# Three stacked attention passes over a graph: the copies of turned rows move from VectorE to ScalarE and wait longer, and a row sum is added up by accumulating transfers

## The chip, the cores and the metric

The kernel runs on one core of one Trainium2 chip, in fp32. The metric is the device time of one execution in microseconds (us); the number given for a kernel is the median of several runs. A profile is one execution taken by the hardware profiler; its span is the time from the first to the last instruction, and its own time is a little longer. The engines are called PE (TensorE), ACT (ScalarE), DVE (VectorE), POOL (GpSimd) and SP (SyncE, which here issues nearly all transfers).

## The reference, cut to what matters

Four residual layers over N = 3327 nodes with 256 features; `adj` is a dense 0/1 matrix. The first three are a cosine attention, a GAT and a query-key attention. The fourth, which the change concerns, is three GAT passes one after the other:

```python
def _gat_layer(h, adj, W, a):
    Wh = h @ W
    f1 = Wh @ a[:F_out]
    f2 = Wh @ a[F_out:]
    e = leaky_relu(f1 + f2.T, ALPHA)
    att = softmax(where(adj > 0, e, NEG_INF), axis=1)
    return elu(att @ Wh)

h = input @ W0
h = _gat_layer(h, adj, W1, a1)      # pass "3a"
h = _gat_layer(h, adj, W2, a2)      # pass "3b"
h = _gat_layer(h, adj, W3, a3)      # pass "3c"
x = layernorm(x + h)
```

## The kernel before, in words

**Tiling.** The nodes are padded to 3328 and cut into 26 tiles of 128 (NT). The rows of the result are cut into 7 blocks (NB): six of 512 (four tiles) and a last one of 256 (two tiles). For a block b and a tile j of source nodes, the attention weights are a 128 x 512 tile. A layer goes over its blocks; in each block over the 26 tiles, in steps j = 0 to 25; PE adds the product of the weights and the tile's values (with a column of ones for the softmax's denominator) into PSUM.

**The weights** of one tile: ACT computes a Relu (L787, `re`), and DVE adds and multiplies by the mask (L800, `ft`). In the deep passes (3a, 3b, 3c; `deep(L)`) four tiles lie in a quad, of which there are three. The weights are made some steps ahead of the products.

**The products** follow Strassen's scheme (`products`, L935) in all blocks of a deep pass but the last: a pair of tiles takes 14 matmuls of 128 x 128, which show as 28 records, instead of 16. For this DVE makes sums of the weights (`quad_sums`, L871 to L874, `qsum`; `sums`, L885, `ssum`), and sums of the values (`combine`, L843 to L853) are stored to memory once per pair of tiles, when the values are made in the pass before; SP fetches them again for each block (`fetch_tsum`, L857, three buffers). The column of ones in such a sum is set by a POOL memset (L843).

**The end of a block** is a generator, `finish`. It runs beside the next block's products, one `yield` per step j (and is run to its end at j = 22). Its parts in a deep pass are: DVE and ACT put the Strassen parts together (`joined`, L961 to L979); ACT divides by the denominators (L1175, L1177); `turn` transposes the block's rows: two ACT copies split the fp32 words into two planes of 16 bits (L990), SP issues a DMA transpose (L993), some yields go by, and two DVE copies put the words together again (L1000, `pT`). PE then projects each of the four tiles by the weights of the pass (L1230, `pproj`, two matmuls a tile); ACT makes the exponential and the Relu of elu (L1239, L1242); and DVE adds them (`activated`, L1254). In the hidden passes (3a and 3b) `follow` then adds the tile to a running sum (`Sum.add`, L1084, one DVE add of 128 x 256), and takes the scores f1 and f2 of the next pass (L719); after each two tiles `combine` makes the next pass's sums. Of block NB-2 the running sum's adds are put off (`L.late`) to after the last block. `Sum.close` (L1088 to L1091) takes the sum across partitions on PE and stores the mean row in the padding row of the values; the values of the whole pass must be there for that.

**How many steps the turned rows wait** is `turn_steps`: 4 in deep passes, at block NB-2 it is 7 (9 in 3c).

**Buffers.** The planes, `pT4` and the tile sums of `combine` share a tag of two buffers ("x4k"). The turned rows lie in one of four "stage" buffers, the elu's exponential in one of two.

**What sets the order.** The code is written as one stream: the step loop calls weights, products and one `advance` of the finishes. A scheduler at build time orders the instructions of each engine's queue from it and places the waits. On the chip each engine works through its queue in order, so an instruction that waits holds up all behind it on that engine.

Of the kernel before, what the change touches and what calls it, by code (L numbers as in the profile page):

```python
# [14 lines left out]
ALU = mybir.AluOpType  # L15
# [18 lines left out]
def gnn_stack(ctx: ExitStack, tc: tile.TileContext, a: dict, N: int, out: bass.AP):  # L34
# [8 lines left out]
    nc = tc.nc  # L43
    NT = (N + P - 1) // P
    NP = NT * P
    NB = (NP + CH - 1) // CH
# [36 lines left out]
    n = 8  # L83
# [549 lines left out]
    def pair_weights(b, p):  # L633
# [16 lines left out]
        def add_two(out, x, ps):  # L650

            nc.vector.tensor_tensor(
                out.rearrange("p (i q) -> p i q", i=2),
                x.unsqueeze(1).to_broadcast([P, 2, D]),
                ps.rearrange("p (i q) -> p i q", i=2),
                add,
            )
# [46 lines left out]
    class Gat:  # L704
        def __init__(self, key):
            self.last = key == "3c"
            self.quads = ("3a", "3b", "3c").index(key) + 1 if key != "1" else 0
            self.k = w.get("k_" + key)
            self.row = w["row_" + key]
            self.sd = cols.tile([P, 2, NT], F32, tag="sd", name="sd")  # L710
            self.th = cols.tile([P, NT], F32, tag="th", name="th")
            self.rh = cols.tile([P, NT], F32, tag="rh", name="rh")
            self.nrh = cols.tile([P, NT], F32, tag="nrh", name="nrh")
            self.u = {}
# [107 lines left out]
    def deep(L):  # L822
        return L.i > 2
# [6 lines left out]
    def combine(key, p, v, e=None):  # L830


        b1, b2 = v[2 * p], v[2 * p + 1]
        b11, b12, b21, b22 = b1[:, H:D], b1[:, :H], b2[:, H:D], b2[:, :H]
        if (key, p) in kept or key == "0":
            t = work.tile([P, 4 * H + 1], F32, tag="tsum", name="tsums", bufs=3)
        else:
            t = work.tile([P, 4 * H + 1], F32, tag="x4k", name="tsum", bufs=2)
        if (key, p) in kept:
            tsums[kept[key, p], p] = t  # L840
        t1, t2, t3, t4 = (t[:, c : c + H] for c in (0, H + 1, 2 * H + 1, 3 * H + 1))
        if e is None:
            nc.gpsimd.memset(t[:, H : H + 1], 1.0)  # L843
            nc.vector.tensor_tensor(t1, b12, b11, ALU.subtract)
            nc.vector.tensor_tensor(t3, b22, b12, ALU.subtract)
        else:
            one = t[:, H : H + 1]
            nc.vector.tensor_scalar(one, e[:, :1], 0.0, None, ALU.is_ge)
            nc.vector.scalar_tensor_tensor(t1, b12, one, b11, ALU.mult, ALU.subtract)
            nc.vector.scalar_tensor_tensor(t3, b22, one, b12, ALU.mult, ALU.subtract)  # L850
        nc.vector.tensor_tensor(t2, b22, t1, ALU.subtract)
        nc.vector.tensor_tensor(t4, t2, b21, ALU.subtract)
        nc.sync.dma_start(t_d[key][p], t)  # L853
# [126 lines left out]
        return z[:, : 2 * q]  # L980


    def turn(x4, n, out, steps=3):

        half = "p k (n t) -> p t k n"
        pl = work.tile([P, 4, 2, D], U16, tag="x4k", name="planes", bufs=2)
        for t in range(2):
            nc.scalar.copy(pl[:, :n, t, :], x4[:, :n, :].bitcast(U16).rearrange(half, t=2)[:, t])  # L990
        yield
        tr = work.tile([P, 16, P], U16, tag="stage", name="turned", bufs=4)
        nc.sync.dma_start_transpose(  # L993
            out=tr[:, : 4 * n, :], in_=pl[:, :n].rearrange("p k t n -> p (k t n)")
        )
        for _ in range(steps):
            yield
        trv = tr[:, : 4 * n, :].rearrange("p (k t h) i -> p t k h i", t=2, h=2)
        for t in range(2):
            nc.vector.tensor_copy(out(t), trv[:, t])  # L1000
        yield

    def turn_steps(L, b):

        if L.key == "1":
            return 5 if b == NB - 2 else 3
        return (9 if L.key == "3c" else 7) if b == NB - 2 else 4

# [64 lines left out]
    class Sum:  # L1075


        def __init__(self):
            self.acc = cols.tile([P, D], F32, tag="xsum", name="xsum")
            nc.gpsimd.memset(self.acc, 0.0)  # L1080

        def add(self, t, x):
            r = LASTP if t == NT - 1 else P
            nc.vector.tensor_tensor(self.acc[:r], self.acc[:r], x[:r], ALU.add)  # L1084

        def close(self, v):
# [6 lines left out]
    def finish(L, b, pos):  # L1093
# [4 lines left out]
        n = len(ts_)  # L1098
# [71 lines left out]
        else:  # L1170
# [23 lines left out]
            if L.key in x_d:  # L1194
                x4 = work.tile([P, 4, D], F32, tag="stage", name="x4", bufs=4)
# [8 lines left out]
            if L.key != "2":  # L1204
                pT4 = work.tile([P, 4, 2, P], F32, tag="x4k", name="pT4", bufs=2)
                yield from turn(
                    p4,
                    n,
                    lambda t: pT4[:, :n].bitcast(U16).rearrange(
                        "p k h (i t) -> p t k h i", t=2  # L1210
                    )[:, t],
                    turn_steps(L, b),
                )
                pTs = {k: pT4[:, k] for k in range(n)}
                if L.key == "1" and b < NB - 2:
                    c4 = work.tile([P, 4, D], F32, tag="x4k", name="c4", bufs=2)
                    yield from projected4(pT4, w[L.w], c4)

            def projected(k):


                if L.key == "2":
                    src = p4[:, k, :]
                elif L.key == "1" and b < NB - 2:
                    src = c4[:, k, :]
                else:
                    pm = bank("pproj")
                    pT = pTs.pop(k)
                    for h in range(2):
                        nc.tensor.matmul(  # L1230
                            pm[:, :D],
                            pT[:, h, :],
                            w[L.w][:, h, :],
                            start=(h == 0),
                            stop=(h == 1),
                        )
                    src = pm[:, :D]
                e = work.tile([P, D], F32, tag="elu_e", name="elu_e", bufs=2)
                nc.scalar.activation(e, src, AF.Exp)  # L1239
                if L.hidden:  # L1240
                    y = work.tile([P, D], F32, tag="y", name="z", bufs=6)
                    nc.scalar.activation(y, src, AF.Relu)  # L1242
                else:
                    y = work.tile([P, D], F32, tag="y", name="y", bufs=6)
                    nc.vector.scalar_tensor_tensor(
                        y, src, 0.0, xr[k], ALU.max, ALU.add
                    )
                es[k] = e
                ys.append(y)

            def activated(k):
                e, y = es.pop(k), ys[k]
                x = nxt[ts_[k]][:, :D] if L.hidden else y
                nc.vector.scalar_tensor_tensor(x, e, 1.0, y, ALU.min, ALU.add)  # L1254
                if L.hidden:
                    follow([k], {k: x})
                else:
                    stats(k)

            for p in range(n + 2):  # L1260
                if p >= 2:
                    activated(p - 2)
                    if b == NB - 2:
                        yield
                    if L.hidden and p % 2 and b < NB - 1:
                        combine(layers[L.i + 1].key, (ts_[0] + p - 3) // 2, nxt)
                if 1 <= p <= n:
                    projected(p - 1)
                if p > 0:
                    yield  # L1270
# [186 lines left out]
    def advance():  # L1457
        while pending:
            try:
                next(pending[0])  # L1460
                return
            except StopIteration:
                pending.popleft()
# [8 lines left out]
    steps = [(L, b, j) for L in layers for b in range(NB) for j in range(NT)]  # L1472
# [79 lines left out]
    for s, (L, b, j) in enumerate(steps):  # L1552
# [146 lines left out]
        if j == NT - 1:  # L1699
            if b == 0 and not last:  # L1700
                nl = layers[L.i + 1]
                L.sum = Sum()
                if nl.is_gat:
                    if nl.key == "1":
                        while "row_1" not in w:
                            next(setup)
                    nl.gat = Gat(nl.key)
                    L.gat_next = nl.gat
            if end:
                pending.append(finish_last(pos[1:], xm, 1))  # L1710
            else:
                pending.append(finish(L, b, pos))
            advance()
# [65 lines left out]
```

## Time and profile before

| | us |
|---|---|
| median of 3 runs | 2300.66 (2299.2 to 2301.87) |
| the profiled execution, its own time | 2297.41 |
| its span | 2295.6 |
| PE busy | 2257.2 (98%) |
| PE weight loads busy | 2004.7 (87%) |
| DVE busy | 1998.3 (87%) |
| ACT busy | 1210.3 (53%) |
| POOL busy | 49.4 (2%) |

Busy times are of one profiled execution. A matmul's end is modelled in the profile and neighbouring matmuls overlap, so the busy time of PE runs ahead of what it could do at its densest pace; starts of records tell more. A group's line names engine, operation, output<-inputs and shape. "[2.23 <-DVE pT L1000]" behind a line of the timeline says that the engine sat idle for 2.23 us, until the named instruction released it. In a table of waits the three numbers are us in total, times, and the longest.

On this time scale the three deep passes lie from about 1380 us to the end: 3a to about 1690, 3b to about 2000, then 3c.

### The profile page before, as it was taken

What the parts mean: (1) busy time and instruction counts of PE and PEld (TensorE: products, weight loads), DVE (VectorE), ACT (ScalarE), POOL (GpSimd) and SP (SyncE); (2) the same over time, 40 slices, a digit from 0 to 9 for tenths busy, and PEclk for the clock granted to TensorE, in tenths of its full rate; (3) what the DMA queues carried; (4) which work ended last, traced back from release to release, by engine and by line L of the source; (5) the groups of instructions that cost most, each with busy time, mean ns of one, the idle gap of its engine ahead of it and who ended that gap; (6) DMA issues with size and microseconds to landing.
All of it is one profiled execution on the core that took longest, in us unless ns stands there. A gap on an engine that the chain in (4) does not pass through costs nothing. (4 is left out here: it accounts for less than half of the span.)

```text
span 2295.6 us, 41529 instructions
## 1 busy us (share of the span) xinstructions
PE 2257.2 (98%) x15183; PEld 2004.7 (87%) x15183; DVE 1998.3 (87%) x5437; ACT 1210.3 (53%) x1982; POOL 49.4 (2%) x196
## 2 busy tenths in 40 slices
PE   9999999999999999999999999999999999999997
PEld 7788888888888877888888899999999999999997
DVE  7789999866777777898898889999899999899996
ACT  4667777764555423223223246555666555655653
POOL 0000001000000000000000000000000000000000
PEclk9999999999999999999999999999999999999999
DMA  8655565523222322132132254444444445355542
GB/s 281 192 178 179 186 195 187 161 84 89 78 72 55 105 61 81 56 100 81 56 99 71 74 171 130 133 136 143 124 129 137 131 134 148 98 152 169 149 122 58
DMA packets 186207, 286.13 MB, mean 125 GB/s; under 512 B 80413, under 2 KB 105492, under 8 KB 181396
## 3 DMA queue, kind: packets, MB, share of 16 engines
q1 hardware_dynamic: 185732, 283.22, 41.2%
q8 instruction: 120, 1.97, 0.4%
q14 instruction: 83, 0.68, 0.1%
q10 hardware_dynamic: 272, 0.26, 0.0%
HBM read 228.21 MB, written 38.44 MB: 116 GB/s over the span
## 5 line engine op out<-in xcount | busy, mean ns | idle before, releaser
L787 ACT ACTIVATE re<-u,nrh,th 128x512 f32<-128x512 f32 (+1 forms) x728 | 539.8, 778 | 343.0 <-DVE ft L800 179.7
L1644 PE MATMUL po<-v,e 128*128 128x257 f32 x1872 | 422.3, 381 | 0.9 <-ACT p L1177 0.8
L1644 PEld LDWEIGHTS po<-v,e 128*128 128x128 f32 x1872 | 352.6, 190 | 60.9 <-issue 9.8
L935 PE MATMUL po<-tsums,qsum 128*128 128x128 f32 (+1 forms) x2520 | 352.8, 275 | 1.4 <-DMA tsums<-t3b_d 0.7
L800 DVE SCALAR_TENSOR_TENSOR ft<-re,rh,mask 128x512 f32<-128x512 f32 x468 | 341.1, 747 | 2.6 <-ACT re L787 2.6
L935 PEld LDWEIGHTS po<-tsums,qsum 128*128 128x128 f32 x2520 | 316.2, 192 | 3.5 <-DVE qsum L873 1.6
L935 PE MATMUL po<-tsums,ssum 128*128 128x128 f32 (+1 forms) x2082 | 293.2, 276 | 4.0 <-DMA tsums<-t3a_d 1.7
L935 PE MATMUL po<-v,ft 128*128 128x129 f32 x1872 | 286.1, 276 | 1.3 <-DVE p L975 0.6
L935 PEld LDWEIGHTS po<-tsums,ssum 128*128 128x128 f32 x2082 | 262.6, 192 | 7.0 <-DVE ssum L885 2.0
L935 PEld LDWEIGHTS po<-v,ft 128*128 128x128 f32 x1872 | 248.2, 192 | 4.0 <-issue 1.8
L935 PEld LDWEIGHTS po<-v,e 128*128 128x128 f32 x1196 | 172.3, 191 | 37.6 <-issue 24.9
L935 PE MATMUL po<-v,e 128*128 128x129 f32 x1196 | 185.1, 275 | 0.0
L800 DVE SCALAR_TENSOR_TENSOR e<-re,rh,mask 128x512 f32<-128x512 f32 (+1 forms) x234 | 149.1, 657 | 38.4 <-PE po L1644 28.4
L524 ACT ACTIVATE ex<-ps,rq 128x512 f32<-128x512 f32 (+1 forms) x183 | 118.9, 652 | 114.7 <-PE ps L511 109.9
L511 PE MATMUL ps<-ft 128*128 128x512 f32 (+1 forms) x364 | 166.9, 564 | 0.0
L496 DVE SCALAR_TENSOR_TENSOR e<-ex,mask 128x512 f32<-128x512 f32 (+1 forms) x182 | 115.8, 650 | 49.0 <-ACT ex L694 27.1
L935 PE MATMUL po<-tsums,ft 128*128 128x128 f32 x936 | 144.2, 275 | 0.0
L525 DVE SCALAR_TENSOR_TENSOR e<-ex,mask 128x512 f32<-128x512 f32 (+1 forms) x183 | 116.8, 644 | 31.1 <-ACT ex L524 30.5
L686 PE MATMUL ps<-gT,ft 128*128 128x512 f32 (+1 forms) x336 | 129.8, 527 | 0.0
L935 PE MATMUL po<-v,qsum 128*128 128x128 f32 x840 | 128.8, 275 | 0.0
L935 PEld LDWEIGHTS po<-tsums,ft 128*128 128x128 f32 x936 | 124.9, 193 | 0.3
L660 ACT ACTIVATE ex<-ex,off 128x512 f32<-128x512 f32 x98 | 67.0, 716 | 101.7 <-DVE ex L676 69.1
(346 smaller groups left out, 3572.8 us busy)
## 6 DMA issues: line engine op xcount, KB each, us to landing
mask<-mask_d SPq DMA_DIRECT2D x30, 1664.0 KB
stage<-in_adj_a SPq DMA_DIRECT2D x78, 512.0 KB
tsums<-t_d SPq DMA_DIRECT2D x152, 256.5 KB
tsums<-t3a_d SPq DMA_DIRECT2D x77, 256.5 KB
tsums<-t3b_d SPq DMA_DIRECT2D x77, 256.5 KB
tsums<-t3c_d SPq DMA_DIRECT2D x77, 256.5 KB
mask_d<-mask SPq DMA_DIRECT2D x6, 1664.0 KB
u<-s_d SPq DMA_DIRECT2D x24, 256.0 KB
```

Source lines behind the costliest of these rows:

```text
L496: nc.vector.scalar_tensor_tensor(e[:, :wd], t_[:, :wd], 0.0, mask(b, j), ALU.add, ALU.mult)
L511: nc.tensor.matmul(ps[:, :wd], FT[j // 4][:, 0, (j % 4) * P : (j % 4 + 1) * P], FT[b][:, 1, :wd], start=True, stop=True,)
L524: nc.scalar.activation(t_[:, c], ps[:, c], AF.Exp, scale=rq[:, j : j + 1])
L525: nc.vector.scalar_tensor_tensor(e[:, c], t_[:, c], 0.0, mask(b, j)[:, c], ALU.add, ALU.mult)
L660: nc.scalar.activation(x[k], x[k], AF.Exp, bias=off, scale=1.0 / D**0.5)
L686: nc.tensor.matmul(ps[:, :wd], FT[j // 4][:, h, (j % 4) * P : (j % 4 + 1) * P], g[:, h, :wd], start=(h == 0), stop=(h == 1),)
L787: nc.scalar.activation(t_[:, :wd], self.u[b][:, :wd], AF.Relu, bias=self.nrh[:, j : j + 1], scale=self.th[:, j : j + 1],)
L800: nc.vector.scalar_tensor_tensor(e[:, :wd], t_[:, :wd], self.rh[:, j : j + 1], mask(b, j), ALU.add, ALU.mult,)
L935: nc.tensor.matmul(o, x, y, start=(p == 0 and g not in banks[:i]), stop=(p == NT // 2 - 1 and g not in banks[i + 1 :]),)
L1644: nc.tensor.matmul(pos[k], e[:, k * P : (k + 1) * P], V[L.i % 2][i], start=(i == 0), stop=(i == NT - 1),)
```

## The change

Four edits, all concerning the deep passes:

- `turn` takes the copying function as an argument; in deep passes the two copies of turned rows (L1000) are made by ACT (`nc.scalar.copy`) instead of DVE.
- `turn_steps` is 7 for all blocks of deep passes (before: 4, and 7 at block NB-2); at block NB-2 of 3c it stays 9.
- In deep passes `finish` yields once more after each `activated`, for all blocks but the last (before: only at block NB-2).
- The running sum made in 3a and 3b is added up by transfers: for the tiles of blocks 0 to NB-3 (20 tiles a pass, 40 in all) POOL issues a transfer that adds the tile into the sum in memory on the chip (`accum_op=add`, 128 KB each). The tiles of the last two blocks are still added by DVE.

```diff
-    def turn(x4, n, out, steps=3):
+    def turn(x4, n, out, steps=3, copy=nc.vector.tensor_copy):
...
         for t in range(2):
-            nc.vector.tensor_copy(out(t), trv[:, t])
+            copy(out(t), trv[:, t])
         yield
 
     def turn_steps(L, b):
 
         if L.key == "1":
             return 5 if b == NB - 2 else 3
-        return (9 if L.key == "3c" else 7) if b == NB - 2 else 4
+        return 9 if L.key == "3c" and b == NB - 2 else 7
...
     class Sum:
-        def __init__(self):
+        def __init__(self, queued):
+            self.queued = queued
             self.acc = cols.tile([P, D], F32, tag="xsum", name="xsum")
             nc.gpsimd.memset(self.acc, 0.0)
 
         def add(self, t, x):
             r = LASTP if t == NT - 1 else P
+            if self.queued and t < 4 * (NB - 2):
+                nc.gpsimd.dma_start(out=self.acc, in_=x, accum_op=ALU.add)
+                return
             nc.vector.tensor_tensor(self.acc[:r], self.acc[:r], x[:r], ALU.add)
...
                     turn_steps(L, b),
+                    nc.scalar.copy if deep(L) else nc.vector.tensor_copy,
                 )
...
                 if p >= 2:
                     activated(p - 2)
-                    if b == NB - 2:
+                    if b == NB - 2 or deep(L) and b < NB - 1:
                         yield
...
-                L.sum = Sum()
+                L.sum = Sum(deep(L))
```

## The prediction

> **What bounds the kernel now.** I read the page's first part, then busy time by stage (windows), the tensor engine's waits, the timeline round the longest of them, and the tiles the change touches.
>
> ```profile
> PE 2257.2 (98%) x15183; PEld 2004.7 (87%) x15183; DVE 1998.3 (87%) x5437; ACT 1210.3 (53%) x1982; POOL 49.4 (2%) x196
> ```
>
> TensorE (PE) is busy for 98% of the span; VectorE (DVE) is next, ScalarE (ACT) has room. By stage (columns: window, its length, then each engine's busy time; four blocks each of layer 2, 3a, 3b and 3c, from join to join):
>
> ```profile
> core 0: us, PE busy (x) PEld busy (x) DVE busy (x) ACT busy (x) POOL busy (x), PEclk, DMA share, GB/s
> 1075.90:1247.80 171.90, 171.76 (x1069) 145.29 (x1068) 152.22 (x467) 50.58 (x94) 0.40 (x4) 1.00 0.24 76
> 1419.80:1604.50 184.70, 178.87 (x1516) 174.93 (x1515) 177.90 (x412) 108.90 (x176) 3.67 (x8) 1.00 0.46 136
> 1722.60:1909.10 186.50, 180.51 (x1511) 176.25 (x1510) 179.44 (x412) 109.74 (x175) 1.37 (x8) 0.98 0.48 135
> 2027.70:2206.30 178.60, 176.65 (x1508) 173.78 (x1507) 176.99 (x406) 106.52 (x156) 0.00 (x0) 1.00 0.52 152
> ```
>
> In 3a to 3c DVE is at 96 to 99%, beside PE at 97 to 99%: two engines at once. What PE could give: one pair of tiles starts every 3.13 us in the undisturbed stretch of 3c (2102.52, 2105.65, 2108.78), so a block of 13 pairs takes 40.7 us, and its 8 projection matmuls (16 records 0.215 us apart) 3.4: 44.1 us. Four are 176.4. The three deep windows exceed that by 8.3, 10.1 and 2.2 us. That is the prize, with the boundaries between the layers: added up over all 18 deep blocks and boundaries from the starts of PE's records, some 34 us. About 10 us more, at the entry to 3a, is not touched. The waits that make it (us in all, times, longest):
>
> ```profile
> PE pproj L1230 <- DVE pT L1000: 12.7, 13, 2.3
> PE po L935 <- DVE ssum L885: 1.4, 2, 0.7
> PE po L935 <- DMA tsums<-t3b_d: 0.9, 2, 0.7
> PE po L935 <- DVE p L975: 0.6, 2, 0.3
> ```
>
> So PE waits in 13 of the 19 finishes for the turned rows. Is DVE late with the copy, or its input? DVE's own waits, then PE and DVE at the longest case (3b, block 3):
>
> ```profile
> DVE pT L1000 <- DMA turned<-planes: 9.7, 9, 2.6
> DVE pT L1000 <- issue: 6.2, 4, 2.4
> ```
>
> ```profile
> 1828.65 0.39 PE L935 MATMUL po<-tsums,ft 128*128 128x128 f32 x2
> 1831.27 4.54 PE L1230 MATMUL pproj<-w_l_w,pT 128*128 128x256 f32 x12 [2.23 <-DVE pT L1000]
> 1835.65 0.38 PE L935 MATMUL po<-tsums,ft 128*128 128x128 f32 x2
> ```
>
> ```profile
> 1829.84 1.37 DVE L1000 COPY pT<-turned 128x1024 uint16<-128x1024 uint16 x2 [2.38 <-issue]
> ```
>
> DVE itself stood still for 2.38 us ahead of the copy: it waited for the transpose, issued at 1823.45, and the copy and PE followed. The wait is mainly the landing, not DVE's load. And three of the four projections stand together here: the 12 merged records last 4.54 us where 12 times 0.215 is 2.6; the granted clock falls after such a stall (the windows' PEclk of 0.98 for 3b). I put that drop at 1.7 us after each of the two longest stalls (2.23 and 2.30 us).
>
> **What the Trainium skill says.** "Perfetto Trace Analysis", Identifying the Most-Contended Engine: busy share of matmuls is a poor measure because they are pipelined; the weight loads' is better. The trace agrees: PE 98% busy, and yet the starts show some 34 us over the dense pace. "VectorE: DVE Perf Modes", The TRN2 errata: ScalarE from SBUF to SBUF costs 224 cycles plus one per element at 1.2 GHz; for 1024 elements 1.04 us, and the same-shaped planes copies on ACT took 1034 ns. "DMA: Bandwidth & Descriptors", SWDGE vs HWDGE vs iDMA: a transfer that accumulates can only be issued by GpSimd; its Anatomy of one DMA gives 2.0 us plus bytes over 436e3 per us, so 2.3 us for 128 KB (an estimate from that page; nothing in this trace shows one). "SBUF — State Buffer", Who interferes with whom: VectorE copies in a two-port mode can shut GpSimd out while it writes descriptors; no run shows it yet, and the change takes the turned-row copies off VectorE.
>
> **The change part by part.** The rows used (ns min/median/max):
>
> ```profile
> L1000 DVE COPY pT<-turned x38: 452/740/757, 1435.4 to 2222.4; 128x1024 uint16<-128x1024 uint16 x34, 128x512 uint16<-128x512 uint16 x4
> ```
>
> ```profile
> L990 ACT COPY planes<-p x40: 602/1034/1046, 1427.3 to 2258.3; 128x1024 uint16<-128x1024 uint16 x36, 128x512 uint16<-128x512 uint16 x4
> ```
>
> ```profile
> L1084 DVE TENSOR_TENSOR xsum<-xsum,v x130: 414/419/434, 118.7 to 2014.0; 128x256 f32<-128x256 f32 x125, 127x256 f32<-127x256 f32 x5
> ```
>
> *Copies to ACT.* 36 big and 4 small copies leave DVE. From start to start one costs 0.68 us: 26 us of DVE with the small ones, plus the part of 9.7 + 6.2 us in which DVE itself stood before them. ACT gains 36 x 1.034 + 4 x 0.60 = 39.6 us, over some 850 us where it is 59% busy (108.9 of 184.7): it becomes no bound. But ACT now waits for the transpose in its place, and the `re` of the next tiles (L787) and the elu exponentials are behind it. In the built order the copies stand after the 18th to 24th `re` of the block, where DVE's stood after the 15th to 18th `ft`; seven steps instead of four put it late enough that the transfer has landed in most blocks (five or six `re` lie between planes and copy, 0.78 us each). Cost on PE's path: 2 x 1.034 against 1.37, so pT is later by 0.7 us in every finish.
>
> *Adds to transfers.* 40 DVE adds leave, 0.419 busy, 0.33 from start to start: 13 us of DVE, in 3a and 3b only. 40 transfers of 128 KB come: 5 MB, beside 130 GB/s over 370 us (48 MB), a tenth more; at 46 to 48% DMA share that hides. They must follow one another, as all add into one tile. The extra yield sets the tiles about two steps, 3.4 us, apart, against the estimated 2.3; if that cover is gone the chain of four (9.2 us) still ends well ahead of the next block's (46 us). The sum is needed only at the layer's end, behind six DVE adds.
>
> *Longer turn, extra yields.* These have no work of their own; they move. In the built order the first projection stands 0 to 6 matmuls later (0 to 1.3 us; I take 0.65), so it cancels the slower copy about; the other three are spread a pair of products apart instead of bunched. The stores of the next layer's tile sums go two or three fetches later in SP's queue, and the memset that starts each stands on Pool behind two accumulations. The last block's finish ends three steps later into the next layer.
>
> *What DVE's relief buys.* DVE drops from about 44.5 to 42 us a block in 3a and 3b, below PE's 44.1. In the first blocks of a layer the join starts late because DVE lags PE: by 3.2, 2.4, 2.3, 1.4 in 3a's blocks 1 to 4, 0.6 twice in 3b, then none, 1.9, 0.7, 0.6, 0.6 in 3c (first join op against PE's last product). A lag that goes brings planes, transpose and copy forward by as much. Taking stall + 0.05 - lag, not below zero, block by block: 3a 0.93, 0.39, 2.09, 1.72 become 0, 0, 0, 0.4; 3b 0.02, 0.23, 2.23, 2.30, 0.66, 0.42 become 0, 0, 2.3, 2.35, 0.7, 0.5; 3c 0.41, 0.29, 0.55 become 0; the boundary keeps 0.5, the end's 0.97 becomes 1.7. From 13.7 (the waits with their short tails) to 8.4.
>
> The sum: waits -5.3; refilling the pipeline after eight stalls that go, 0.16 each, -1.3; half of the two clock drops, -1.7; the small DVE-lag waits (ssum, p L975 and the like, with what the starts show round them), -3.0; against them +1.5, my middle between 0 (all hidden) and 3 (a late tile sum, as tsums rows above, once more in four blocks at 0.7) for Pool's and SP's longer chains. Net -9.8 us: 2297.4 - 9.8 = 2287.6 for the profiled execution (span 2295.6, 1.8 outside). The median of the runs is 3.25 higher, so I say 2291.
>
> **The rivals.** *All of it goes:* spread projections and a spare DVE end every stall: 13.7 + 12 x 0.16 + 3.4 + 5 = 24 us, 2277. For: seven steps (7 x 3.13 / 2 = 11 us) outlast every landing shown (6.6 us). Against: pproj hardly moves in PE's queue. *Nothing measurable:* the landing chain (9.5 to 11.5 us from join to planes, 4.3 to 6.6 to land, then the copy) sets pproj; the copy's 0.7 on 19 finishes is 13 us and eats the gain: 2296 to 2305, about 2300. *Slower:* ACT is the place. A copy that waits there holds the `re` behind it, DVE's `ft` starve and PE follows. The order needs DVE ahead by about ten steps instead of six over the first blocks of a layer: four `ft` at 0.67 and four quad sums at 0.61, 5.1 us of lead. DVE gains 42 against 44.1 only if it isn't starved; below about 1.7 us gained a block it has not the lead in three blocks, and PE waits some 5 us more a layer: 15 us in three layers, less the gain of 5: 2310. The changed queue order speaks for it; that ACT has 40% idle against it. That the accumulation doesn't leave DVE isn't open: the instruction is replaced.
>
> **How the numbers follow.** Modest gain, 5 to 17 us, 2291: 0.55. All of it, 2277: 0.13. Hidden, within 0.2% (4.6 us, about what a measurement of this kernel can tell from no change): 0.16. Slower, 2310: 0.16. Faster by over 0.2% is then 0.68. The range 2279 to 2306 leaves out some 0.08 below and 0.11 above; the gain case alone is 2284 to 2296.
>
> **What would show it.** Right: DVE busy in the 3b window down by some 10 us and ACT up by 8; waits of pproj, now for ACT, 8 to 9 us in all, mostly in 3b's blocks 3 and 4; deep windows near 180, 182 and 177. Wrong: pproj waits of 15 us or more (the copy's 0.7 counted everywhere); `ft` on DVE waiting for `re` behind the copies, which shows 2.6 us now; products waiting for `ft` or for tile sums by more than 5 us; accumulating transfers above 3.4 us each, so that Pool's memsets come late.

## The result, and the profile after

The changed kernel takes 2314.19 us (median of 4 runs, 2313.33 to 2314.81) against 2299.93 us of the kernel before: a ratio of 1.0063, 95% interval 1.0047 to 1.0079. It is slower by 14 us (the interval of the ratio makes 11 to 18 of it), where I had forecast 10 us faster; the time lies outside my range.

The changed kernel's own profiled execution took 2313.90 us, with this first part of its page and these windows of four blocks (columns as before: window, length, busy time of each engine):

```profile
span 2312.1 us, 41648 instructions
...
PE 2259.0 (98%) x15183; PEld 2006.6 (87%) x15183; DVE 1968.2 (85%) x5357; ACT 1252.1 (54%) x2022; POOL 77.7 (3%) x236
```

```profile
core 0: us, PE busy (x) PEld busy (x) DVE busy (x) ACT busy (x) POOL busy (x), PEclk, DMA share, GB/s
1421.00:1611.90 190.90, 180.42 (x1516) 177.68 (x1516) 173.57 (x395) 120.02 (x188) 14.84 (x24) 0.98 0.55 143
1733.60:1918.90 185.30, 178.90 (x1511) 175.57 (x1510) 172.91 (x391) 120.75 (x185) 14.57 (x24) 0.99 0.57 147
2039.50:2220.30 180.80, 177.25 (x1515) 174.50 (x1514) 174.08 (x398) 114.80 (x164) 0.00 (x0) 1.00 0.53 152
```

The change did what it says: VectorE is busy 30 us less, ScalarE 42 us more. VectorE now has slack: in 3a it is busy for 91% of the window, where it was 96%. And still 3a's four blocks take 6.2 us longer and 3c's 2.2; 3b's are 1.2 shorter. That is 7.2 us of the 16.5 by which the profiled span grew; the rest lies in the stretches between and around these windows, at the boundaries of the passes. PE's instructions are the same (15183 in both), so it waits more. These are the waits of PE in the deep passes of the changed kernel (us in all, times, longest):

```profile
PE pproj L1235 <- ACT pT L1000: 16.1, 14, 2.1
PE po L935 <- DMA tsums<-t3a_d: 5.0, 4, 3.7
PE po L935 <- DVE ft L800: 3.5, 3, 2.1
PE po L935 <- DMA tsums<-t3b_d: 2.8, 3, 1.5
PE po L935 <- DVE p L975: 1.5, 4, 0.6
PE po L935 <- DMA tsums<-t3c_d: 1.0, 1, 1.0
```

Two things stand out. The projections wait for the turned rows 16.1 us, not less than the 12.7 before. And the products wait for fetched tile sums 8.8 us (5.0 + 2.8 + 1.0), where it was 1.7. (The products also wait 3.5 us for `ft`, in three stalls; ahead of the two longest VectorE was busy without a gap, so it was late itself.) For the first, see the row of the copies:

```profile
L1000 ACT COPY pT<-turned x40: 752/1334/1360, 1436.5 to 2280.7; 128x1024 uint16<-128x1024 uint16 x36, 128x512 uint16<-128x512 uint16 x4
```

The median is 1334 ns. I had taken 1034, the row of the planes, which has the same engine, shape and type. The pair of copies takes 2.5 us from start to end, where VectorE's took 1.37. One finish, in 3a, on ACT and then on PE in the changed kernel:

```profile
1581.60 2.52 ACT L1000 COPY pT<-turned 128x1024 uint16<-128x1024 uint16 x2 [1.56 <-DMA turned<-planes]
```

```profile
1584.17 1.13 PE L1235 MATMUL pproj<-w,pT 128*128 128x256 f32 x4 [2.06 <-ACT pT L1000]
```

ACT stands for 1.56 us until the transpose lands, copies for 2.52, and PE starts as soon as that ends. Here the copy doesn't queue behind other work: its whole length is on PE's path. Only 4 records of `pproj` stand together now instead of 12, as the change intends.

The second, at the longest wait, on SP's queue and on PE:

```profile
1496.69 0.32 SPq L857 DMA_DIRECT2D tsums<-t3a_d  x1
1503.12 0.32 SPq L427 DMA_DIRECT2D mask<-mask_d  x1
1503.54 0.37 SPq L857 DMA_DIRECT2D tsums<-t3a_d  x1
1504.83 0.32 SPq L853 DMA_DIRECT2D t3b_d<-tsum  x1
1505.26 2.00 SPq L857 DMA_DIRECT2D tsums<-t3a_d  x2
```

```profile
1511.84 1.44 PE L935 MATMUL po<-tsums,qsum 128*128 128x128 f32 x5 [3.71 <-DMA tsums<-t3a_d]
```

L427 is the fetch of the next block's mask, 1664 KB, once a block. SP stood at it for six microseconds, by the profile for an instruction of VectorE. The next fetch of tile sums stands directly behind it. In the trace's transfer records the mask's packets run from 1504.07 to 1510.27, and the tile sums behind them land 7 us after their issue, where the median of pass 3a is about 2.6. There are three buffers for tile sums and a pair of tiles takes 3.13 us, so there is little room for 7 us. Late landings alone aren't new, though: in the kernel before, too, the fetches behind a mask landed after up to 6.6 us in the deep passes, and PE waited only 1.7 us for tile sums. In the changed kernel the latest took 8.0.

### The profile page after: what moved, and what is told of

The parts are those of the page before. It is cut to its first block, busy times and chain, and to the rows that moved or that the text cites. A ratio compares the mean times of both kernels' runs of the same rounds, so it can differ in the third digit from the quotient of the medians.

```text
span 2312.1 us, 41648 instructions
## 1 busy us (share of the span) xinstructions
PE 2259.0 (98%) x15183; PEld 2006.6 (87%) x15183; DVE 1968.2 (85%) x5357; ACT 1252.1 (54%) x2022; POOL 77.7 (3%) x236
## 4 chain that ended last, share of the span: by engine, by line
PE 71%; DVE 13%; DMA 7%; ACT 6%; issue 2%; POOL 0%; SPq 0%; DVEq 0%; ACTq 0%; POOLq 0%
PE po L935 32%; PE po L1649 15%; PE ps L647 6%; PE ps L511 6%; PE ps L686 5%; DMA turned<-planes 3%; DVE ft L800 3%; PE pproj L1235 2%; ACT pT L1000 2%; ACT re L787 1%; ACT planes L990 1%; PE pv L1318 1%; DMA tsums<-t3a_d 1%; PE pgq L541 1%; DVE ejunk L719 1%
```

## The experiments

The theories tested, under the names that the expectations use. A: ScalarE's slow copies make pT late (P once it was combined with Q; P1 if it is their length by the output's form, P2 if their place in ScalarE's queue). B: the accumulating transfers make the tile sums late (later Q; Q1 by GpSimd's queue, Q2 by load on the DMA engines). C: the longer finish itself makes them late (later R; M once the mask fetch was named as the means).

Ratios are to the kernel before, run beside on the same chip, and so is the difference of the medians in the third column (the medians of the kernel before were 2299.9 us beside the change and 2297.4 to 2298.5 us beside the others). Times of different rows come from different chips; the text compares them by this third column. The waits are those of PE in the deep passes, from each one's profile: for pT at `pproj` (that of the very last finish, 1 to 2 us, is left out in most), and for tile sums at the products. In split_copy 7.9 of the 12.7 stand in the view under `ft`, in store_pool and acc_memset 0.9 and 0.8 under `tsum`; PE starts there 0.05 to 0.06 us after the end of the copy of pT, as in the others. The waits are of one execution each: those profiled of only_acc, contig_half and u_yield took 3 to 4 us more than their medians, that of after_mask_half 4 us less.

| | median us | to the kernel before, us | ratio (95% interval) | pT | tile sums |
|---|---|---|---|---|---|
| before | 2299.93 | 0 | 1 | 12.7 | 1.7 |
| the change | 2314.19 | +14.3 | 1.0063 (1.0047 to 1.0079) | 16.1 | 8.8 |
| u_copy | 2300.59 | +2.1 | 1.0008 (1.0000 to 1.0016) | 6.1 | 10.2 |
| u_steps | 2313.34 | +14.8 | 1.0056 (1.0043 to 1.0068) | 24.1 | 2.8 |
| u_yield | 2307.42 | +8.9 | 1.0039 (1.0023 to 1.0054) | 19.9 | 4.7 |
| u_acc | 2307.91 | +9.4 | 1.0036 (1.0024 to 1.0048) | 20.3 | 1.1 |
| only_copy | 2312.07 | +14.5 | 1.0063 (1.0050 to 1.0076) | 24.4 | 1.7 |
| only_acc | 2294.87 | -3.1 | 0.9988 (0.9981 to 0.9995) | 13.1 | 3.1 |
| steps_yields | 2295.79 | -1.8 | 0.9992 (0.9983 to 1.0000) | 6.2 | 6.4 |
| split_copy | 2303.96 | +6.4 | 1.0029 (1.0017 to 1.0040) | 12.7 | 5.4 |
| copy_contig | 2300.06 | +2.1 | 1.0010 (1.0003 to 1.0016) | 11.5 | 9.9 |
| memset_dve | 2307.09 | +9.5 | 1.0044 (1.0031 to 1.0056) | 20.5 | 0.4 |
| acc_memset | 2299.29 | +1.3 | 1.0010 (1.0002 to 1.0018) | 7.2 | 8.6 |
| store_pool | 2297.72 | -0.3 | 1.0002 (0.9994 to 1.0010) | 9.5 | 5.0 |
| sy_mask_half | 2292.68 | -5.8 | 0.9977 (0.9971 to 0.9984) | 5.4 | 0.0 |
| sy_mask_pool | 2305.06 | +6.6 | 1.0028 (1.0016 to 1.0041) | 9.3 | 2.0 |
| after_mask_half | 2308.24 | +9.8 | 1.0042 (1.0029 to 1.0055) | 19.4 | 3.3 |
| contig_half | 2296.20 | -1.2 | 0.9995 (0.9987 to 1.0003) | 14.0 | 4.0 |
| before_mask_half | 2300.36 | +2.9 | 1.0014 (1.0008 to 1.0021) | 17.1 | 0.0 |
| sy_acc_half | 2295.36 | -2.1 | 0.9992 (0.9984 to 1.0000) | 6.2 | 0.0 |

### One part of the change taken back

**u_copy.** The copies go back to VectorE.

```diff
-                    nc.scalar.copy if deep(L) else nc.vector.tensor_copy,
+                    nc.vector.tensor_copy,
```

> The changed kernel with the two copies of turned rows back on VectorE; everything else of the change stays. Theory A (ScalarE copies are slow, 1.33 us each in the new profile instead of the 1.03 I took, and hold up ScalarE's queue): about 2300 us, 14 us below the changed kernel. Theory B (the accumulating transfers delay the tile sums): stays at 2314. Theory C (the later finish puts stores and fetches late in SP's queue): about 2310, since the copies are not the cause, and projections still wait for pT.

From 14.3 to 2.1 us above the kernel before: most of the loss is gone. Its waits of PE:

```profile
PE pproj L1235 <- DVE pT L1000: 6.1, 7, 1.5
PE po L935 <- DMA tsums<-t3a_d: 5.0, 3, 2.7
PE po L935 <- DMA tsums<-t3b_d: 4.5, 4, 2.1
```

The wait for pT is 10 us less than with ScalarE's copies, and half of what it was in the kernel before; but the tile sums take that gain away.

**u_steps.** The old four steps.

```diff
-        return 9 if L.key == "3c" and b == NB - 2 else 7
+        return (9 if L.key == "3c" else 7) if b == NB - 2 else 4
```

> The changed kernel with the old waits of turned rows, four steps. Theory A: 5 to 15 us slower than 2314, as ScalarE would stand longer before a transpose that hasn't landed. Theory B: 2314. Theory C: 3 to 8 us faster, about 2308.

No difference in time (1.0056 against 1.0063): waits for pT rise by 8 us, those for tile sums fall by 6. Neither theory A nor C had the exchange.

**u_yield.** No extra yields.

```diff
-                    if b == NB - 2 or deep(L) and b < NB - 1:
+                    if b == NB - 2:
```

> The changed kernel without the extra yields after each activated tile. Theory A: 2314, unchanged. Theory B: the four accumulations come two steps closer together (1.5 us apart where one takes over 2), so slower by up to 5 us. Theory C: the finish ends four steps earlier, faster by 5 to 10 us, about 2306, with tile-sum waits of products back to 2 us from 9.

About 5 us faster, and the tile-sum waits nearly halved, as theory C has it, while those for pT rise by 4. Its runs scatter more than the others' (2302.8 to 2317.2), so the size is less sure.

**u_acc.** All adds back on VectorE.

```diff
-                L.sum = Sum(deep(L))
+                L.sum = Sum(False)
```

> The changed kernel with all running-sum adds back on VectorE (0.42 us each, 40 of them). Theory A: 2314 to 2318. Theory B: about 2302, with the gain all in passes 3a and 3b. Theory C: 2314 to 2318, slower rather than faster, as VectorE has 13 us more to do.

About 5 us faster, with tile-sum waits of 1.1 us (and pT's up by 4): the transfers have a part in those for tile sums. The four differences (12, 0, 5 and 5 us) add up to one and a half times the loss: the parts overlap.

### One part of the change alone

The edits are the same, in the other three places. **only_copy** has the copies alone:

> Only the copies go to ScalarE, the waits stay at four steps, no extra yields, adds on VectorE. Theory P: about 2310, with pproj waits of some 25 us; the copies alone cost about 10 us. Theory R: about 2300, the copies alone are harmless.

It is as slow as the whole change. Theory P holds: the copies alone cost as much, and the only wait of PE that grew by more than 1.5 us is that for pT (24.4 us, 12.7 before). **only_acc** has the transfers alone:

> Only the accumulating transfers, all else as before. My prediction's step (VectorE's 13 us less bring the joins forward and take 5 to 8 us of waits): about 2292. Theory Q1 (the memsets stand behind the transfers): 2300 to 2304, with tile-sum waits of 5 us or more.

It is a little faster than before, 3 us. But in its profiled execution the wait for pT didn't fall:

```profile
PE pproj L1235 <- DVE pT L1000: 13.1, 13, 2.5
```

VectorE has 13 us less to do, and PE waits for the turned rows as long as ever (12.7 before). This execution was no faster than that of the kernel before, so where the 3 us of the median come from it doesn't show. **steps_yields** has the longer wait and the extra yields, with the copies and adds where they were:

> Only the longer wait of the turned rows and the extra yields; copies and adds on VectorE as before. Theory P plus Q (two faults that hide a gain: ScalarE's copies make pT late, the accumulating transfers make tile sums late; the longer finish by itself takes pT's waits away): about 2290 us, pproj waits at most 6 us and tile-sum waits at most 2 us. Theory R (the longer finish is itself what makes the tile sums late): 2298 or more, with tile-sum waits of 5 us or more.

```profile
PE pproj L1235 <- DVE pT L1000: 6.2, 6, 1.8
PE po L935 <- DMA tsums<-t3a_d: 3.6, 3, 2.2
PE po L935 <- DVE p L975: 3.4, 7, 0.8
...
PE po L935 <- DMA tsums<-t3c_d: 1.7, 2, 1.0
```

So in this profile the longer finish halves the wait for pT by itself, without any relief of VectorE; 6.5 us won. Tile sums (+4.7) and the joins (`p`, L975, +2.8) take it back. This lies between the two theories: R is right on the waits, and the time is 1.8 us below the kernel before, at the edge of what can be told.

### Why the copies are long

**split_copy.** One copy on each engine.

```diff
-            copy(out(t), trv[:, t])
+            (copy if t else nc.vector.tensor_copy)(out(t), trv[:, t])
```

> The changed kernel with one of the two copies on VectorE and the other on ScalarE, side by side. If the length of the copies counts (2.6 us on ScalarE against 1.4 on VectorE before), pT is ready after 1.3 us and pproj waits fall from 16 to about 7 us: 2305 or less. If it is ScalarE's queue (the copy stands behind work there), little changes: 2310 to 2314.

8 us faster than the whole change, though the pT waits fell only by 3.4. It speaks for the length, not as clearly as I had hoped. **copy_contig** changes where the words are written; both copies also read the plane of the high halves, so the low halves are left out:

```diff
-            copy(out(t), trv[:, t])
+            copy(out(t), trv[:, 1 if copy == nc.scalar.copy else t])
...
-                        "p k h (i t) -> p t k h i", t=2
+                        "p k h (t i) -> p t k h i" if deep(L) else "p k h (i t) -> p t k h i", t=2
```

> The changed kernel with ScalarE's copies writing their 16-bit words side by side instead of every second one; both copies take the plane of the high halves, so pT holds other numbers than the reference needs (the low halves are left out). It does the same number of elements. Theory P1 (the copy is long because of its interleaved output, and its length stands on PE's path in each finish): the copies take 1.03 us like those of the planes, pT is ready 0.6 us sooner in 16 to 18 finishes, 8 us faster, about 2306, pproj waits some 8 us. Theory P2 (it is where the copy stands in ScalarE's queue): 2312 to 2314. If the copies take 1.33 us all the same, the output's form isn't the reason for their length.

```profile
L1000 ACT COPY pT<-turned x40: 601/1041/1046, 1435.1 to 2265.8; 128x1024 uint16<-128x1024 uint16 x36, 128x512 uint16<-128x512 uint16 x4
```

The same number of elements takes 1041 ns, and the time falls from 14.3 to 2.1 us above the kernel before. The copies stand for the same landing as ever (18.7 us of waiting for `turned` in 12 cases, 18.0 in the changed kernel), so their place is not what made the difference: theory P1. 0.6 us a finish, in some 18 finishes, makes 11 us, close to the 12. It doesn't come as shorter waits alone, though; more of that under "Settling the account".

### Why the tile sums are late

**memset_dve.** The memset ahead of each tile sum goes from GpSimd to VectorE.

```diff
-            nc.gpsimd.memset(t[:, H : H + 1], 1.0)
+            (nc.vector if key in ("3b", "3c") else nc.gpsimd).memset(t[:, H : H + 1], 1.0)
```

> The changed kernel with the memset of the column of ones (24 of them) on VectorE, so that GpSimd's queue holds the accumulating transfers alone. Theory Q1 (the memset stands behind accumulating transfers in GpSimd's queue and makes the tile sums, and SP's stores and fetches behind them, late): about 2308, as without the transfers, and products wait for tile sums for 2 us or less. Theory Q2 (the transfers load the DMA engines and delay other transfers, whatever the queue): stays at 2314, waits for tile sums near 9 us.

About 5 us faster, tile-sum waits almost gone (0.4 us) and pT's up by 4, with the transfers all still there: it looked like GpSimd's queue, Q1, and not like Q2. **acc_memset** is the same edit with the copies on VectorE:

> The change without ScalarE's copies and with the memset of the column of ones on VectorE: longer wait, extra yields and accumulating transfers. If the accumulation is harmless once GpSimd's queue holds no memset, the 13 us that VectorE no longer works buy something: 2290 to 2293, below the longer finish alone (2295.8). If they buy nothing: 2295 to 2297. If the load on the DMA engines counts: 2299 to 2301.

Here it gains only 1 us over u_copy, and the products go on waiting 8.6 us. So the memset behind the transfers isn't the general cause; what it changed beside ScalarE's slow copies isn't shown, and the gain of 5 us there is not much more than the uncertainty of the changed kernel's own time. **store_pool** is steps_yields with the memset on VectorE and the stores of tile sums issued by GpSimd:

```diff
-        nc.sync.dma_start(t_d[key][p], t)
+        (nc.gpsimd if key in ("3b", "3c") else nc.sync).dma_start(t_d[key][p], t)
```

> The longer wait and the extra yields alone, with the stores of tile sums issued by GpSimd instead of SP, and the memset on VectorE. Theory R (after the longer finish a store that waits for VectorE holds up the fetches behind it in SP's queue): waits for tile sums fall from 6.4 us to 2 or less, about 2291. If the waits stay, the fetches are late for another reason (mask or row fetches): 2296.

Tile-sum waits of 5.0 instead of 6.4, no gain: theory R, in the form that the stores hold up SP's queue, falls. What is left is the mask fetch, ahead of nearly every late fetch in the traces. **sy_mask_half** is steps_yields with that fetch in two halves, at steps 8 and 12:

```diff
-        elif j == 8 and not (last and b == NB - 1):
+        elif j in ((8, 12) if deep(L) else (8,)) and not (last and b == NB - 1):
             nb = (b + 1) % NB
-            masks[nb] = fetch_mask(nb)
+            h = NT * bw(nb) // 2
+            if not deep(L):
+                masks[nb] = fetch_mask(nb)
+            elif j == 8:
+                masks[nb] = new_mask(nb)
+                nc.sync.dma_start(masks[nb][:, :h], mask_d[nb][:, :h])
+            else:
+                nc.sync.dma_start(masks[nb][:, h : 2 * h], mask_d[nb][:, h : 2 * h])
```

> The longer wait and the extra yields alone (2295.8 before), with the mask fetch of 1664 KB, one a block in the deep passes, split in two halves four steps apart. Theory M (a fetch of tile sums that SP issues right behind the mask's stands behind its 1.66 MB on the DMA engines and lands after 4 to 7 us instead of 2.5, and the longer finish pushes stores between the two, so that it starts later): waits for tile sums fall from 6.4 us to 2 or less, 2290 to 2293. If the fetches are late for another reason: 2296.

```profile
PE pproj L1235 <- DVE pT L1000: 5.4, 8, 1.4
PE po L935 <- DVE p L975: 3.9, 9, 0.8
PE po L935 <- ACT re L787: 3.3, 7, 0.8
```

No wait for tile sums is left, and the kernel is faster than before beyond doubt, by 0.23%. It was the landing, and not SP's standing at the mask: by the waits of SP's queue it stood there 20.7 us in all in steps_yields and still 21.3 here, at the first halves, while the latest fetch of tile sums in the deep passes landed after 5.3 us instead of 7.1. Next in line are the joins and ScalarE's `re`, with short waits. **sy_mask_pool** gives the whole fetch to GpSimd instead:

```diff
-            masks[nb] = fetch_mask(nb)
+            masks[nb] = fetch_mask(nb, nc.gpsimd if deep(L) else nc.sync)
```

> The longer wait and the extra yields alone, with the whole mask fetch issued by GpSimd, on another queue, in the deep passes. Theory M, as far as it is the order in SP's queue: as with the halves, 2290 to 2293. If two queues share the DMA engines packet by packet and the mask's packets delay the tile sums all the same: 2296, with waits for tile sums as they were.

The tile-sum waits fall to 2.0 us, as they should if it is the place in SP's queue; but the kernel is slower, and products now wait for weights (`ft`, 7.3 us in two stalls). The mask isn't late, VectorE waits for none in this trace. The two stalls lie at the two boundaries between the passes, and this is what VectorE does just ahead of them:

```profile
DVE ri L1193 <- PE po L1649: 8.6, 2, 4.3
```

It waits for the old pass's last products, to divide by their denominators, and what it needs for the next pass's first weights stands behind that in its queue. In steps_yields those come first, and there is no such wait. The edit to the mask fetch has changed the built order of another queue.

**after_mask_half** has the split in the whole changed kernel:

> The whole changed kernel (2314.2) with the mask fetch in two halves. Theory M: its waits for tile sums, 8.8 us, fall to 3 or less; 2306 to 2309. If the accumulating transfers alone make them late: 2314.

About 4.5 us faster, at the edge of what can be told; tile-sum waits 3.3 instead of 8.8.

### Settling the account

**contig_half** is the changed kernel with copy_contig's and sy_mask_half's edits:

> The whole changed kernel with both faults taken out: ScalarE's copies write side by side (both take the high halves, the low ones are left out, so the numbers are not the reference's), and the mask fetch is halved. If the two failed steps are the whole of the prediction's miss: 2314.2 less 14.1 for the copies and 6 for the mask, about 2294, within 3 us of the predicted 2291. If they overlap, because a late pT gave the tile sums time: 2297 to 2300.

From 14.3 above the kernel before to 1.2 below it: the two faults are 15.5 of the 24 us by which I missed (I had forecast 9.7 below); they overlap a little (12 and 4.5 apart). Its pT waits are 14.0 us. **before_mask_half** has the split alone:

> The kernel before with nothing but the mask fetch in two halves. It waits for tile sums only 1.7 us, so if theory M is right, 2296 to 2298, within 0.2% of it. If halving the mask is worth 5 us by itself, the longer finish is worth nothing: 2293.

```profile
PE pproj L1235 <- DVE pT L1000: 17.1, 14, 2.6
```

No gain, 3 us of loss. PE may be sooner at the turned rows where no tile sum holds it up, but the wait there grew by 4.4 us and only 1.7 had gone, so that isn't all of it. The split was worth something only with the longer finish, and the longer finish little without the split. **sy_acc_half** adds the accumulating transfers:

> Longer wait, extra yields and accumulating transfers, copies on VectorE, the mask fetch in two halves. If the 13 us that leave VectorE are worth what they were worth alone (3 us): about 2290, the fastest of all. If VectorE isn't on the path any more, or the transfers delay the tile sums: 2293 or more.

2.1 us below the kernel before, against 5.8 without them: once the finish is long and the mask split, they cost rather than save. sy_mask_half is the fastest kernel of all that ran.

**What the waits leave out.** The waits of PE that the views list don't give the times by themselves. From the changed kernel to copy_contig they fall from 30.2 to 23.8 us in all, and the profiled span by 15.2. Much of the rest is PE's granted clock. After the stall of 3.71 us shown above, the windows (columns as before, PEclk third from the end) have:

```profile
1511.80:1515.20 3.40, 3.36 (x15) 3.36 (x16) 2.31 (x4) 1.27 (x2) 0.00 (x0) 0.50 0.35 130
1515.20:1518.60 3.40, 3.40 (x33) 3.40 (x32) 2.71 (x10) 2.55 (x4) 0.00 (x0) 1.00 0.30 77
```

Half the clock for 3.4 us is 1.7 us lost. In the deep passes the kernel before has two such stretches, the changed kernel three, only_copy five, copy_contig and sy_mask_half none. In all 20 profiled executions, what the listed waits (1400 to 2276 us) and these losses differ from the kernel before gives the difference of the span to within 3.6 us (correlation 0.98; 0.88 for the waits alone). For sy_mask_half the waits are 1.8 us less and the losses 3.4, together the 5.2 us by which its span is shorter.

## Why the prediction was wrong, point by point

- **What bounds the kernel:** right. PE sets the end, by its waits for the turned rows, and the landing of the transpose is the main part of these. The one run in which only VectorE had less to do (only_acc) didn't shorten them in its profile. That PE's busy share of 98% was a poor measure here is not shown: 34 us over the dense pace are 1.5% of the span, about what the share leaves.
- **Copies to ACT, "pT is later by 0.7 us in every finish":** this step failed, and it decides the sign. The price of 1.034 came from the nearest row and was borne out by the Trainium skill's formula ("VectorE: DVE Perf Modes", The TRN2 errata), which counts elements and not how they lie. The copies measured 1.334; with the words side by side they fell to 1.041. The pair takes 2.52 us against VectorE's 1.37, so pT is later by 1.15 us. The sum had set the 0.7 off against 0.65 us by which the first projection would stand later, and so charged 0.05 a finish. The wrong length alone is worth 12 of the 14 us (copy_contig).
- **Longer turn, extra yields:** I named the stores that go later in SP's queue and gave them 1.5 us in the sum, "my middle between 0 (all hidden) and 3". Tile-sum waits rose from 1.7 to 8.8 us in the profile. The mechanism was near (SP's order), the object wrong: not the stores, but the mask fetch that I didn't mention. It takes 6 us of transfer and stands ahead of the fetches. Splitting it is worth some 4.5 us in the changed kernel.
- **"What DVE's relief buys", 13.7 to 8.4 us:** this failed too. steps_yields reaches 6.2 with no relief; only_acc has relief and stays at 13.1. It is the longer finish that shortens this wait; which of its two parts, the later copies or the spread projections, no run takes apart with VectorE's copies. With both faults taken out the whole change still waits 14.0, 5.6 us above my 8.4, and its time is 8.5 us above the forecast.
- **The clock:** that a drop costs 1.7 us was right. I counted on 1.7 us less of it ("half of the two clock drops"); the changed kernel has three drops in place of two, so 1.7 us more.
- **Adds to transfers:** harmless alone (only_acc gains 3 us). Their own time was wrong: the page estimate of 2.3 us from issue to landing ("DMA: Bandwidth & Descriptors", Anatomy of one DMA) met a median of 4.1 in this trace. That they hide "at 46 to 48% DMA share" failed with the longer finish, where they cost some 4 us (sy_acc_half).
- **The rivals.** The slower one had the sign and the place, ScalarE, and a time near the measured one (2310), but not the mechanism. VectorE's wait of `ft` for `re` went only from 2.6 to 4.9 us, and copy_contig puts the loss down to the copy's length, not to ScalarE's queue. "Nothing measurable" was right to count the copy's length in every finish; it used 0.7 us, and copy_contig, with copies as short as that, took the time that it gives, about 2300. So with the copies as I had priced them the gain would still not have come.
- **The signs I had named:** of those for "wrong", three came true: waits at `pproj` of 15 us or more (16.1), waits for tile sums of more than 5 (8.8), and transfers above 3.4 us each (4.1).

What stays open: by what the accumulating transfers add to the waits for tile sums (u_copy against steps_yields, 10.2 to 6.4), why moving the memset helps beside ScalarE's copies, and the 8.5 us that are left of the miss with both faults out, beyond the 5.6 us of waits for pT in that run's profile.

## What to carry to other kernels

A copy priced by "the same engine, shape and type" needs the same order of its output too; look for a row with the same pattern, or take the longer bound. Where a chain ends in an engine that is waiting, moving its last link to an idle but slower engine can cost the difference at every turn, however much room that engine has. When work in a queue is moved, list the large transfers of that queue: a short fetch directly behind a long one landed late by most of the long one's time here (7 us instead of 2.6, behind 6.2 us of transfer), and cutting the long one in two can be what turns a move from nothing into a gain. And look at the longest stalls first: those of two microseconds and more often cost more here than they lasted.

## What the runs showed of the hardware

The interleaved output costs ScalarE 28% (1334 against 1041 ns for 1024 16-bit elements a partition), and VectorE's copies of the same pattern take 740.

The clock: in the 20 traces, between 1400 and 2276 us, PE has 388 stalls of 0.3 to 1.8 us, and the granted clock fell to half after none of them. After 20 of the 42 stalls of 1.8 to 2.2 us it did, and after 19 of the 23 longer ones, each time for 3.4 us (three times for 6.8); it fell nowhere else in that stretch. What decides among the stalls near 2 us isn't shown.

An accumulating transfer of 128 KB occupies GpSimd for 0.86 us,

```profile
L1086 POOL DMA_DIRECT2D xsum<-v x40: 852/859/1172, 1441.8 to 1958.7; - x40
```

and lands after 4.1 us, median (2.6 at the least). Each of its packets of 1024 bytes holds a DMA engine for 102 ns (median in 3a and 3b), more than the 85 ns of the tile sums' packets of 2052 bytes: per byte more than twice as much. Plain packets differ too, though (those of `u`, of 2048 bytes, take 104), and whether it is the adding that costs, or another thing of this transfer, no run separates.
